# A decoder's self-attention with its projection groups in another place, some of its evictions on VectorE alone, and the first block's groups in another order

## The chip, the core and the metric

The kernel runs on one core of a Trainium2 chip. A core has five engines with a queue of instructions each: TensorE (PE; its weight loads are shown as PEld), VectorE (DVE), ScalarE (ACT), GpSimd (POOL) and SyncE (SP, which here issues all the transfers). Each works through its queue in order and waits at an instruction until semaphores of other engines or of transfers have come. The metric is the device time of one execution in microseconds (us); lower is better. Three runs of the kernel before gave 3051.44, 3047.96 and 3051.34 us; their median is 3051.34 us.

## The reference

A transformer encoder layer works on a context of 77 rows, and a decoder layer on 2048 rows, for 2 batches; width 512, 16 heads of 32 channels, feed-forward width 2048, all in float32. Cut to what matters here:

```python
x = src + mha(ln(src), ln(src), enc weights, eb);  memory = x + ff(ln(x))      # 77 rows a batch
yn = ln(tgt)                                                                    # 2048 rows a batch
y  = tgt + mha(yn, yn, dec_sa weights, rel_bias + causal)                       # the change is here
y  = y + mha(ln(y), memory, dec_ca weights, cb)
y  = y + relu(ln(y) @ ff1.T + b1) @ ff2.T + b2

def mha(xq, xkv, ...):
    q, k, v = xq @ wq.T + bq, xkv @ wk.T + bk, xkv @ wv.T + bv                  # 16 heads of 32
    attn = softmax(q @ k.T / sqrt(32) + bias)
    return (attn @ v) @ w_out.T + b_out
```

## The kernel before

The first part of the program, some 1865 us of it, is the decoder's self-attention, with the encoder and the first block's cross-attention fitted in between. The second part (cross-attention and feed-forward) is not touched by the change.

**Units, pieces, blocks.** The 2048 queries of a batch are cut into 4 *blocks* m of 512, numbered x = 0 to 7 over both batches (x = 4b + m); a block has 16 *units* (b, m, g, t): a group g of 4 heads and a tile t of 128 queries, in this order, so that there are 128 units n in all. By the causal mask tile i = 4m + t sees i + 1 tiles of 128 keys, which `pieces` (L292) cuts into pieces of at most four: one piece for m = 0, two for m = 1, three for m = 2, four for m = 3. The last piece of a unit has as many key tiles as are left: with m > 0 it is 2 for t = 0 and t = 1, 3 for t = 2 and 4 for t = 3.

A piece j of unit n passes through three steps:

- `scores(n, j)` (L325): four matmuls, one for each head, into four banks of PSUM. DVE evicts each bank to the buffer `pp` and takes the maximum (L352; L359 with the bias on the last two tiles); after the last piece DVE negates the maximum (L366) and ACT exponentiates each head's whole row (L367), four instructions a unit.
- `turn(n, j)` (L373): PE transposes the probabilities, 128x128 each (L387); every bank of four is copied to SBUF as `pts`, by ACT (L393), or, for the last piece of a unit, by DVE (L391; with one piece, ACT and DVE in turn). For the first piece the groups go by heads, so that the first waits for the first exponential alone; for later pieces they go by key tiles.
- `values(n, j)` (L396): PE multiplies the values with `pts` (L406) into a bank of its own, number 7. After the last tile of a head group ACT copies it out as `oT` (L412).

All other matmul groups take the seven other banks in turn (`bank`, L168).

**The projections.** For each block there are 16 jobs, each a group of 4 matmuls of 128x512 that the profile shows as 8: `q_job` (evicted by DVE, L206), `k_job` (evicted by ACT, L216), `v_job` (DVE, L229) and `out_job` (DVE, L241, and a store by SP). Small steps ("light") go with them: the loads, statistics, centring and the transposes of the next block's normal form (`norm_load`, `norm_stats`, `norm_center`, `norm_turn`; the four transposed tiles are scaled and shifted to `nT` by DVE and ACT in turn, L289 and L287), the division by the sums (`divide`), the encoder's 28 stages (one for each slot from 0 on, L942) and the first cross-attention (from slot 64 on, L956).

**What sets the order.** It is written out by hand. `jobs[n]` and `light[n]` list what goes into `slot(n)` (L948), at fixed distances from the block's first unit u = 16x (L877 to L903): a slot of a middle block has one job. The weights of a job are loaded by a transfer that is put into SP's queue earlier: two jobs are loaded at the start (L920), and each job that runs loads the next one of the list (L954), so that SP stands two jobs ahead. The last loop (L1199) gives the order of each engine's queue:

```python
for n in range(end):
    slot(n)
    for j in range(pn):
        turn(n, j)
        scores(n + 1, j + 1)     # or, for the last j: what unit n + 1 has more, and scores(n + 2, 0)
        values(n, j)
```

So the projection of slot n stands between `values` of the unit before and the first transposes of unit n. `scores(n + 1, k)` for k from pn on exist only where a unit has more pieces than the one before it: at the first unit of blocks 1, 2, 3, 5, 6 and 7.

Of the kernel before, what the change touches and what calls it, by code (L numbers as in the profile page):

```python
# [11 lines left out]
AF = mybir.ActivationFunctionType  # L12
ALU = mybir.AluOpType
# [7 lines left out]
NC = D // P  # L21
NF = DFF // P
HC = P // HD
MB = 512
# [30 lines left out]
def tile_encoder_decoder(ctx: ExitStack, tc: tile.TileContext, ins, out):  # L55
    nc = tc.nc
    x, src = ins["x"], ins["ctx_1024"]
# [19 lines left out]
    def vec(name, i):  # L77
        c = _COL[name] + i
        return vecs[:, c : c + 1]
# [67 lines left out]
    with (  # L147
# [6 lines left out]
        kT = ac.tile([P, NC, T], F32, name="kT")  # L154
# [13 lines left out]
        def bank():  # L168

            i = count["bank"] % count["banks"]  # L170
            count["bank"] += 1
            return psum[:, i, :]
# [13 lines left out]
        def small_w(c0, name="dec_sa_in_wT"):  # L186
            w = sb.tile([P, NC, P], F32, name="wqk", tag="wqk", bufs=3)
            nc.sync.dma_start(w, wchunk(name, c0, P))
            return w

        def big_w(kind, b, m):
            if wbig.get("is") != (kind, b, m):
                w = wbt
                nc.sync.dma_start(
                    w, wchunk("dec_sa_in_wT", 2 * D) if kind == "v" else wchunk("dec_sa_out_wT", 0)
                )
                wbig["is"], wbig["w"] = (kind, b, m), w
            return wbig["w"]

        def q_job(b, m, g):  # L200
            def run(w):
                mm = bank()
                for c in range(NC):
                    nc.tensor.matmul(mm, w[:, c, :], nTs[b, m][:, c, :], start=(c == 0), stop=(c == NC - 1))
                q = sb.tile([P, MB], F32, name="q", tag="q", bufs=3)
                nc.vector.tensor_scalar(q, mm, vec("dec_sa_in_b", g), SCALE, ALU.add, ALU.mult)  # L206
                qTs[b, m, g] = q

            return lambda: small_w(g * P), run

        def k_job(b, m, g):
            def run(w):
                mm = bank()
                for c in range(NC):
                    nc.tensor.matmul(mm, w[:, c, :], nTs[b, m][:, c, :], start=(c == 0), stop=(c == NC - 1))  # L215
                nc.scalar.activation(  # L216
                    kT[:, g, ts(m, MB)], mm, AF.Identity, bias=vec("dec_sa_in_b", NC + g)
                )

            return lambda: small_w(D + g * P), run  # L220

        def v_job(b, m, t):
            def run(w):
                mm = bank()
                for c in range(NC):
                    nc.tensor.matmul(
                        mm, nTs[b, m][:, c, ts(t, P)], w[:, c, :], start=(c == 0), stop=(c == NC - 1)
                    )
                nc.vector.tensor_tensor(vv[:, m * TB + t, :], mm, bv, ALU.add)  # L229

            return lambda: big_w("v", b, m), run
# [40 lines left out]
        def norm_turn(b, m, t, apart=False):  # L272
            xn = xs.pop((b, m, t))
            if t == 0:
                nTs[b, m] = nTt
            nT = nTs[b, m]

            pts = [bank()] * NC
            if apart:
                pts[0] = bank()  # L280
            for c in range(NC):
                nc.tensor.transpose(pts[c][:, ts(c, P)], xn[:, ts(c, P)], ident)
            for c in range(NC):
                d, pt = nT[:, c, ts(t, P)], pts[c]
                sc, bi = vec("dec_n1_s", c), vec("dec_n1_b", c)
                if c % 2 or (apart and c):
                    nc.scalar.activation(d, pt[:, ts(c, P)], AF.Identity, bias=bi, scale=sc)  # L287
                else:
                    nc.vector.tensor_scalar(d, pt[:, ts(c, P)], sc, bi, ALU.mult, ALU.add)  # L289
# [16 lines left out]
        units = [(b, m, g, t) for b in range(B) for m in range(NMB) for g in range(NC) for t in range(TB)]  # L306
# [66 lines left out]
        def turn(n, j):  # L373

            k0, kn = parts[n][j]
            p = state[n]["p"]
            pn = len(parts[n])
            got = {}
            if j == 0:
                order = [[(r, k) for k in range(kn)] for r in range(HC)]  # L380
            else:
                order = [[(r, k) for r in range(HC)] for k in range(kn)]
            for o, group in enumerate(order):
                pt = bank()
                pts = in_turn("pts", pts_all).rearrange("p (x q) -> p x q", q=P)
                for x, (r, k) in enumerate(group):
                    nc.tensor.transpose(pt[:, ts(x, P)], p[r][:, ts(k0 + k, P)], ident)  # L387
                    got[r, k] = pts[:, x, :]
                w = len(group) * P
                if j == pn - 1 and (pn > 1 or o % 2):  # L390
                    nc.vector.tensor_copy(pts[:, : len(group), :], pt[:, :w])  # L391
                else:
                    nc.scalar.copy(pts[:, : len(group), :], pt[:, :w])  # L393
            state[n]["pts"] = got
# [475 lines left out]
        jobs = {n: [] for n in range(-1, len(units) + NU)}  # L870
        light = {n: [] for n in range(-1, len(units) + NU)}

        for x, (b, m) in enumerate(blocks):
            u = x * NU
            first = m == 0

            jobs[u if first else max(u - 3, -1)].append(v_job(b, m, 0))  # L877
            jobs[u + 1 if first else u - 2].append(v_job(b, m, 1))
            jobs[u + 1].append(v_job(b, m, 2))
            jobs[u + 2].append(v_job(b, m, 3))  # L880
            jobs[max(u - 5, -1)].append(q_job(b, m, 0))
            jobs[max(u - 4, -1)].append(k_job(b, m, 0))
            jobs[max(u - 1, 0)].append(q_job(b, m, 1))
            jobs[u].append(k_job(b, m, 1))
            for g, at in ((2, 3), (3, 5)):
                jobs[u + at].append(q_job(b, m, g))
                jobs[u + at + 1].append(k_job(b, m, g))
            for t in range(TB):
                end = x == len(blocks) - 1
                jobs[u + NU + (2 if end else 7) + t].append(out_job(b, m, t))  # L890
                at = u + NU + ((-1, 0, 3, 4)[t] if end else 6 + t)
                light[at].append(lambda b=b, m=m, t=t: residual(b, m, t))
                if x:
                    light[u - NU + 4 + t].append(lambda b=b, m=m, t=t: norm_load(b, m, t))
                    light[u - NU + 5 + t].append(lambda b=b, m=m, t=t: norm_stats(b, m, t))
                    light[u - NU + 6 + t].append(lambda b=b, m=m, t=t: norm_center(b, m, t))
                    light[u - NU + 7 + t].append(lambda b=b, m=m, t=t: norm_turn(b, m, t))
            for g in range(NC):
                d = divide(b, m, g)
                for k in range(2):  # L900
                    light[u + g * TB + TB + k].append(lambda d=d: next(d, None))
                at = u + g * TB - 3
                light[max(at, -1)].append(lambda b=b, m=m, g=g: load_bias(b, m, g))  # L903
# [12 lines left out]
        def load_next():  # L916
            if len(loaded) < len(queue):
                loaded.append(queue[len(loaded)][0]())

        load_next()  # L920
        load_next()
        v = pp[:H, 13056 : 13056 + 3 * LT].rearrange("h (m u) -> h m u", u=LT)
        make_bias(1, rel, v)
        row_into(bv, "sa_bv")
# [23 lines left out]
        def slot(n):  # L948
            for f in light[n]:
                f()  # L950
            for _, run in jobs[n]:
                run(loaded[ran[0]])
                ran[0] += 1
                load_next()  # L954

        for r, fs in first_cross().items():  # L956
            light[len(units) // 2 + r] += fs


        w_1 = pp[:, : END // 2].rearrange("p (c o) -> p c o", c=NC)  # L960
# [235 lines left out]
            scores(0, j)  # L1196
        scores(1, 0)
        end = len(units)
        for n in range(end):  # L1199
            slot(n)  # L1200
            pn = len(parts[n])
            for j in range(pn):
                turn(n, j)
                if n + 1 < end:
                    nx = len(parts[n + 1])
                    if j < pn - 1:
                        if j + 1 < nx:
                            scores(n + 1, j + 1)
                    else:
                        for k in range(pn, nx):  # L1210
                            scores(n + 1, k)
                        if n + 2 < end:
                            scores(n + 2, 0)
                values(n, j)
# [61 lines left out]
```

## Time and profile before

| | |
|---|---|
| median of three runs | 3051.34 us (3047.96 to 3051.44) |
| profiled execution | 3047.41 us, span 3045.6 us, mean granted clock of TensorE 0.989 |
| self-attention, 0 to 1865.4 us of the span | PE busy 1803.09, DVE 1245.49, ACT 1122.47, POOL 91.24 us |
| the rest, 1865.4 to 3045.6 us | PE busy 1140.79, DVE 788.53, ACT 261.29, POOL 644.82 us |
| first transposes of blocks 0 to 7 | 46.7, 196.8, 424.0, 668.6, 979.9, 1118.0, 1326.2, 1570.8 us |

A row of the timeline gives start, duration, engine, line, instruction, tiles, shape and how many were merged; in square brackets stands the idle time of the engine before it and what ended it. A row of the waits gives engine, tile and line, what it waited for, then the sum, the number and the longest in us. A row of a table of stretches gives the length and, for PE, PEld, DVE, ACT and POOL, the busy time and in brackets the instructions, then the granted clock (1.00 is full) and the share and speed of the transfers. A matmul's end is modelled, so a PE row that is merged over a short wait counts that wait as busy: what PE loses is read from the starts.

### The profile page before, as it was taken

Reading aid. Unit: us, or ns where it says so; the run is one execution under the profiler, and the core shown is the slowest. Engines: PE = TensorE matmul, PEld = TensorE weight load, DVE = VectorE, ACT = ScalarE, POOL = GpSimd, SP = SyncE. Lnnn points to the kernel's source line nnn. Section 1 sums busy time; section 2 is a strip of 40 time slices with the busy share of each in tenths; the row PEclk is TensorE's granted clock in tenths of the full one; section 3 lists DMA queues with packets and bytes.
Section 4 is the critical chain, followed back from the end, with each engine's and each line's share of the span. In section 5 each row is a group of like instructions: output and inputs, shape, how many; then the busy total and the mean of one; then the engine's idle time right before and its main releaser. Section 6 shows DMA issues by size and latency. Waiting matters only on the chain. (4 is left out here: it accounts for less than half of the span.)

```text
span 3045.6 us, 60835 instructions
## 1 busy us (share of the span) xinstructions
PE 2943.9 (97%) x24440; PEld 2033.0 (67%) x24440; DVE 2034.0 (67%) x5863; ACT 1383.8 (45%) x2527; POOL 736.1 (24%) x601
## 2 busy tenths in 40 slices
PE   8899999999999999999999998999999999999999
PEld 5566656666665555656666665687778677778788
DVE  4766567766765777767666663676767666767765
ACT  2444466667776545566667773213131213131211
POOL 0100000000000101000000001464656454656465
PEclk9899999999999999999999999999999999999999
DMA  6413301201012421201101113200001000000000
GB/s 157 109 48 108 96 22 46 60 22 40 26 43 61 100 56 60 72 24 50 57 19 33 40 36 102 90 28 1 28 1 37 9 28 1 28 1 28 1 15 14
DMA packets 117644, 137.11 MB, mean 45 GB/s; under 512 B 18240, under 2 KB 73072, under 8 KB 117234
## 3 DMA queue, kind: packets, MB, share of 16 engines
q1 hardware_dynamic: 117362, 133.22, 15.3%
q8 instruction: 193, 3.16, 0.4%
q14 instruction: 89, 0.73, 0.1%
HBM read 111.33 MB, written 21.86 MB: 44 GB/s over the span
## 5 line engine op out<-in xcount | busy, mean ns | idle before, releaser
L352 DVE TENSOR_SCALAR_CACHE_REDUCE pp<-psum 128x512 f32<-128x512 f32 (+3 forms) x1024 | 560.6, 590 | 292.7 <-PE psum L343 292.7
L367 ACT ACTIVATE pp<-pp,nm 128x128 f32<-128x128 f32 (+15 forms) x512 | 610.6, 1194 | 152.3 <-DVE nm L366 149.5
L393 ACT COPY pts<-psum 128x512 f32<-128x512 f32 (+3 forms) x816 | 408.7, 581 | 418.9 <-PE psum L387 410.1
L387 PEld LDWEIGHTS psum<-ident,pp 128*128 128x128 f32 x4352 | 481.3, 142 | 119.7 <-issue 97.6
L387 PE MATMUL psum<-ident,pp 128*128 128x128 f32 x4352 | 544.6, 276 | 14.3 <-ACT pp L367 12.0
L1076 POOL TENSOR_TENSOR vv<-pp 128x512 f32<-128x512 f32 x320 | 413.0, 1307 | 149.2 <-PE psum L1093 129.9
L406 PEld LDWEIGHTS psum<-pts,vv 128*32 128x32 f32 x8704 | 219.0, 110 | 271.0 <-issue 146.4
L343 PE MATMUL psum<-kT,q 32*128 32x512 f32 (+3 forms) x2560 | 382.5, 579 | 4.6 <-ACT nT L287 1.6
L406 PE MATMUL psum<-pts,vv 128*32 128x128 f32 x8704 | 341.1, 279 | 30.8 <-DVE pts L391 28.1
L1112 ACT ACTIVATE kT<-kT,vecs 128x256 f32<-128x256 f32 x256 | 115.2, 499 | 322.3 <-DVE kT L1109 322.3
L359 DVE CUSTOM_DVE_ANT_0 pp<-psum,bias 128x256 f32<-128x256 f32 (+1 forms) x512 | 209.8, 410 | 60.0 <-PE psum L343 60.0
L264 POOL TENSOR_TENSOR rstd<-rstd,mhalf 128x1 f32<-128x1 f32 x32 | 18.5, 577 | 893.2 <-DVE rstd L263 893.2
L391 DVE COPY pts<-psum 128x512 f32<-128x512 f32 (+3 forms) x328 | 195.5, 645 | 52.8 <-PE psum L387 51.8
L1109 DVE TENSOR_TENSOR kT<-kT,psum 128x512 f32<-128x512 f32 x256 | 166.2, 679 | 83.1 <-PE psum L1093 83.1
L343 PEld LDWEIGHTS psum<-kT,q 32*128 32x128 f32 x2560 | 134.7, 183 | 81.8 <-issue 45.5
L1123 PE MATMUL psum<-vv 128*128 128x256 f32 x768 | 176.9, 381 | 0.0
L249 POOL TENSOR_TENSOR xr<-xr,row_dec_sa_out_b 128x512 f32<-128x512 f32 x32 | 40.9, 1280 | 525.5 <-DMA xr<-in_x_dram 246.7
L1093 PE MATMUL psum<-oT,vv 128*128 128x256 f32 x736 | 166.8, 380 | 0.0
L1123 PEld LDWEIGHTS psum<-vv 128*128 128x128 f32 x768 | 143.1, 190 | 26.8 <-issue 9.5
L1093 PEld LDWEIGHTS psum<-oT,vv 128*128 128x128 f32 x736 | 138.7, 190 | 24.8 <-issue 6.7
L1076 DVE TENSOR_TENSOR vv<-kT 128x512 f32<-128x512 f32 x160 | 140.9, 898 | 10.8 <-PE psum L1123 9.9
L215 PE MATMUL psum<-nT,wqk 128*128 128x512 f32 x256 | 120.3, 614 | 6.1 <-DMA wqk<-in_dec_sa_in_wT_dram 6.0
(167 smaller groups left out, 3922.8 us busy)
## 6 DMA issues: line engine op xcount, KB each, us to landing
wqk<-in_dec_sa_in_wT_dram SPq DMA_DIRECT2D x64, 256.0 KB, 4.3
bias<-tz SPq DMA_DIRECT2D x128, 128.0 KB, 3.6
wbig<-in_dec_sa_in_wT_dram SPq DMA_DIRECT2D x8, 1024.0 KB, 8.0
vv<-in_enc_ff_wT_dram SPq DMA_DIRECT2D x8, 1024.0 KB, 5.3
wbig<-in_dec_sa_out_wT_dram SPq DMA_DIRECT2D x8, 1024.0 KB, 10.0
xr<-in_x_dram SPq DMA_DIRECT2D x32, 256.0 KB, 4.5
y<-xr SPq DMA_DIRECT2D x32, 256.0 KB, 2.7
vv<-y SPq DMA_DIRECT2D x32, 256.0 KB, 3.5
```

Source lines behind the costliest of these rows:

```text
L343: nc.tensor.matmul(banks[r][:, : kn * P], q[rows4(r), ts(t, P)], kT[rows4(r), g, k0 * P : (k0 + kn) * P], start=True, stop=True,)
L352: nc.vector.tensor_scalar(p[:, k0 * P : (k0 + far) * P], s[:, : far * P], 1.0, None, ALU.mult, ALU.max, accum_out=st["mx"][:, r, c : c + 1],)
L359: nc.vector.tensor_tensor_reduce(p[:, (i + 1) * P - w : (i + 1) * P], s[:, far * P : kn * P], biases[b, m, g][:, r, 2 * P - w :], 1.0, LOW ...
L367: nc.scalar.activation(p[:, : (i + 1) * P], p[:, : (i + 1) * P], AF.Exp, bias=nm, accum_out=sums_of[b, m, g][:, t, r : r + 1],)
L387: nc.tensor.transpose(pt[:, ts(x, P)], p[r][:, ts(k0 + k, P)], ident)
L391: nc.vector.tensor_copy(pts[:, : len(group), :], pt[:, :w])
L393: nc.scalar.copy(pts[:, : len(group), :], pt[:, :w])
L406: nc.tensor.matmul(ot[rows4(r), t, :], vv[:, k0 + k, ts(g * HC + r, HD)], got[r, k], start=(k0 + k == 0), stop=(k0 + k == nb - 1),)
L1076: engine.tensor_tensor(dst, quarter(*parts[0], n), quarter(*parts[2], n), SIGN[parts[1]])
L1093: nc.tensor.matmul(mm[:, ts(f, TOK)], a[:, c, ts(f, P)], b[:, c, :], start=(c == 0), stop=(c == 1))
L1109: nc.vector.tensor_tensor(dst, dst, got, SIGN[sign])
L1123: nc.tensor.matmul(mm[:, t, :], lhs[:, c, ts(t, P)], rhs[:, c, :], start=(n == 0 and c == 0), stop=(n == 3 and c == 1),)
```

## The change

It does seven things: `slot(n + 1)` is called behind the last `turn` of unit n, ahead of the scores and the values that follow it, instead of ahead of unit n + 1; `norm_turn` leaves all four evictions to DVE (but for block 0); `k_job` evicts by DVE in blocks 2, 3, 6 and 7; the jobs of block 0 stand in other slots, and the v jobs of block 4 one or two slots later; three jobs are loaded at the start instead of two, so that the first v weights go into SP's queue ahead of the relative bias's write to DRAM; the two jobs of slot 4 load nothing, so that SP stands one job ahead from there on; and the first cross-attention begins one slot later.

```diff
@@ k_job
-                nc.scalar.activation(
-                    kT[:, g, ts(m, MB)], mm, AF.Identity, bias=vec("dec_sa_in_b", NC + g)
-                )
+                d, bi = kT[:, g, ts(m, MB)], vec("dec_sa_in_b", NC + g)
+                if m >= 2:
+                    nc.vector.tensor_scalar(d, mm, bi, None, ALU.add)
+                else:
+                    nc.scalar.activation(d, mm, AF.Identity, bias=bi)
@@ norm_turn
-                if c % 2 or (apart and c):
+                if apart and c:
                     nc.scalar.activation(d, pt[:, ts(c, P)], AF.Identity, bias=bi, scale=sc)
                 else:
                     nc.vector.tensor_scalar(d, pt[:, ts(c, P)], sc, bi, ALU.mult, ALU.add)
@@ the lists of jobs
-            jobs[u if first else max(u - 3, -1)].append(v_job(b, m, 0))
-            jobs[u + 1 if first else u - 2].append(v_job(b, m, 1))
-            jobs[u + 1].append(v_job(b, m, 2))
-            jobs[u + 2].append(v_job(b, m, 3))
+            jobs[u + 1 if first else max(u - 3, -1)].append(v_job(b, m, 0))
+            jobs[u + 2 if first else u - 2].append(v_job(b, m, 1))
+            jobs[u + 3 if first else u + 1].append(v_job(b, m, 2))
+            jobs[u + 4 if first else u + 2].append(v_job(b, m, 3))
             jobs[max(u - 5, -1)].append(q_job(b, m, 0))
             jobs[max(u - 4, -1)].append(k_job(b, m, 0))
-            jobs[max(u - 1, 0)].append(q_job(b, m, 1))
-            jobs[u].append(k_job(b, m, 1))
-            for g, at in ((2, 3), (3, 5)):
+            jobs[u - 1 if x else 2].append(q_job(b, m, 1))
+            jobs[u if x else 3].append(k_job(b, m, 1))
+            for g, at in ((2, 3), (3, 5)) if x else ((2, 4), (3, 5)):
                 jobs[u + at].append(q_job(b, m, g))
                 jobs[u + at + 1].append(k_job(b, m, g))
@@ the loads ahead
-        load_next()
-        load_next()
+        for _ in range(3):
+            load_next()
@@ slot
                 ran[0] += 1
-                load_next()
+                if n != 4:
+                    load_next()
 
         for r, fs in first_cross().items():
-            light[len(units) // 2 + r] += fs
+            light[len(units) // 2 + 1 + r] += fs
@@ the last loop
+        slot(0)
         for n in range(end):
-            slot(n)
             pn = len(parts[n])
             for j in range(pn):
                 turn(n, j)
+                if j == pn - 1 and n + 1 < end:
+                    slot(n + 1)
                 if n + 1 < end:
                     nx = len(parts[n + 1])
```

## The prediction

> **What bounds the kernel now.** First the head of the page, then the table of stretches for self-attention and for one middle block, then the waits.
>
> ```profile
> span 3045.6 us, 60835 instructions
> PE 2943.9 (97%) x24440; PEld 2033.0 (67%) x24440; DVE 2034.0 (67%) x5863; ACT 1383.8 (45%) x2527; POOL 736.1 (24%) x601
> ```
>
> ```profile
> 0.00:1865.40 1865.40, 1803.09 (x17880) 1140.93 (x17882) 1245.49 (x4510) 1122.47 (x2014) 91.24 (x98) 0.99 0.22 60
> 1326.20:1570.80 244.60, 241.13 (x2569) 152.61 (x2568) 170.12 (x612) 162.88 (x267) 7.23 (x8) 1.00 0.14 40
> ```
>
> ```profile
> PEld psum L406 <- DVE pts L391: 110.3, 174, 3.6
> PE psum L406 <- DVE pts L391: 28.1, 85, 3.3
> PE psum L387 <- ACT pp L367: 12.0, 13, 1.3
> PE psum L215 <- DMA wqk<-in_dec_sa_in_wT_dram: 6.0, 1, 6.0
> ```
>
> TensorE sets the end. Its 97% hides waits, because merged rows count short ones as busy; the weight loads of L406, which wait 110.3 us in 174 places for the copies of DVE, show them better. Block 2, unit 38 (t = 2, three key tiles in its last piece) in PE's timeline:
>
> ```profile
> 518.83 1.14 PE L343 MATMUL psum<-kT,q 32*128 32x512 f32 x8
> 519.90 1.08 PE L406 MATMUL psum<-pts,vv 128*32 128x128 f32 x32
> 520.91 1.53 PE L387 MATMUL psum<-ident,pp 128*128 128x128 f32 x12
> 522.37 2.20 PE L343 MATMUL psum<-kT,q 32*128 32x512 f32 x8
> 524.50 0.78 PE L406 MATMUL psum<-pts,vv 128*32 128x128 f32 x16
> 525.45 0.43 PE L406 MATMUL psum<-pts,vv 128*32 128x128 f32 x8 [0.17 <-DVE pts L391]
> 525.80 0.66 PE L282 MATMUL psum<-ident,xt 128*128 128x128 f32 x4
> 526.29 3.60 PE L238 MATMUL psum<-wbig,oT 128*128 128x512 f32 x8
> ```
>
> Undisturbed scores take 1.07 (518.83 to 519.90), those behind the last transposes 2.13; the values take 1.30 (524.50 to 525.80) where 24 of them take 0.79. PE loses 1.57 us, while DVE empties the score banks of the next unit and copies `pts`; then a projection of 3.44 us (8 x 0.43) follows that needs neither.
>
> **The projection moved (the main term).** It falls between the last transposes and the scores, so DVE has 3.44 us more before PE needs it. Read so, from start to start, units of blocks 2 and 6 lose 0.28, 1.09, 1.57 and 0.09 us there for t = 0 to 3: 3.03 a head group, 12.1 a block; the last unit, 1.4 more, and unit 40 bring it to 13.7. Slots 61, 62 and 123 to 127 have no job and give nothing back; the other units of blocks 1 to 7 lose, in this order, 13.3 + 13.7 + 11.6 + 11.5 + 12.2 + 13.7 + 7.5 = **83.5 us**. In block 0 units 6 to 10 are DVE's: 24.5 of 28 us busy between 100 and 128, where the wait only changes place; I take 3 there and read 4.5 in its other units: **7.5**.
>
> **Who waits next: ACT.** The first transposes now follow the values at once, and need the exponentials.
>
> ```profile
> 1683.43 1.88 ACT L367 ACTIVATE pp<-pp,nm 128x1920 f32<-128x1920 f32 x1
> 1685.22 0.18 ACT L367 ACTIVATION_READ_ACCUMULATOR pp<-pp,nm 128x1 f32 x1
> 1685.33 0.69 ACT L216 ACTIVATE kT<-psum,vecs 128x512 f32<-128x512 f32 x1
> 1685.92 2.04 ACT L393 COPY pts<-psum 128x512 f32<-128x512 f32 x4
> ```
>
> Unit 118's transposes start at 1685.13, its fourth head's group 1.31 later, 1.13 after the exponential's end (1685.31). The slot only moves within the same distance, so this slack shrinks just by the stall removed. In blocks 1 and 2 it is 2.8 us or more: nothing lost. In blocks 3 and 7 it is 1.1 to 1.7 for t = 2 and 3, against 1.09 and 1.57 removed; ACT's four copies (2.05) then start some 0.6 late and the values wait 0.55: eleven such units, **-6**. L412's copy (0.56) now runs in front of these copies without the projection to cover it: mostly inside their slack, **-1**.
>
> At the first units of blocks 1, 2, 3, 5, 6, 7 the unit's own last scores come behind the slot. Block 3: 0.95 from the scores to the first negated maximum, four exponentials at 1.67, L412, copies: 0.95 + 6.7 + 0.56 + 2.05 = 10.3, where the values would stand at 5.6 (scores 1.7, values 1.0, transposes 1.84, scores 1.07). That is 4.7, and 1.46 is lost there today: 3.3. In the same way 3.4 for m = 2 and 1.8 for m = 1; twice each: **-17**. The cover for this used to be the projection.
>
> **Evictions on DVE.** Normal form: 28 tiles, two more DVE instructions each of 0.407 (L289): 22.8 us of DVE, ACT rid of 56 x 0.456. Keys: 16 x 0.69 (L216, and L229 on DVE 0.687) = 11 us. The Trainium skill (TensorEngine Tiling (Array Packing), "PSUM Bottleneck") advises to evict with ScalarE and VectorE both; by it the change costs up to 22.8 + 11 = 34 us. The row says otherwise for the normal form: in one bank the two took turns, and ACT waited 40.0 us for L289, DVE 18.8 for L287. A tile held DVE 1.34 us with its wait (133.93 to 135.27, block 0); DVE starts its next instruction 0.33 after an L289 (115.41 to 115.73), so four come to 1.3 to 1.6. So DVE pays 0 to 8, and the key eviction stands where DVE waits for the projection anyway, as q's does. Were that cover gone: 11. With self-attention 66 us shorter DVE is 71% busy; in blocks 4 and 5 it goes from 75% to 81 to 85%, and I take **-5** (0 to -25). On ACT the key would have stood behind the four exponentials, and a bank with it.
>
> **Block 0's order.** Today PE waits 6.0 us for one k weight, and then runs at half clock:
>
> ```profile
> 34.55:40.52 5.97, 0.00 (x1) 0.04 (x1) 0.75 (x1) 0.00 (x0) 0.00 (x0) 0.89 0.92 200
> 40.52:46.91 6.39, 6.39 (x10) 2.76 (x11) 0.00 (x0) 0.00 (x0) 0.00 (x0) 0.57 0.01 2
> 107.50:110.90 3.40, 0.58 (x10) 0.19 (x5) 3.31 (x5) 0.01 (x1) 1.27 (x2) 0.99 0.00 0
> 110.90:117.70 6.80, 6.27 (x68) 5.04 (x69) 5.01 (x23) 3.98 (x12) 0.28 (x1) 0.50 0.77 86
> ```
>
> That job moves from slot 0 to slot 3. PE gets there near 50: first transposes done 27.8, v 3.4, scores to transposes 2.4, v, q and the encoder's transposes 7.5, again 3.2, the encoder's q 2.1, v 3.4. Its transfer, at 27.24 today, now stands behind the four bias pieces and a 768 KB bias write (8 us at the 95 GB/s of 9 to 15 us), with the 1 MB v weight gone from in front: landing 46 to 49. So **+8.8** (6.0, and 6.39 - 3.60; 5 if it lands late). The v weight passes SP's bias write and delays it by about 2 us; the first bias is needed at 25.7, its load lands near 25: 0 to -1.5, I take 0.
>
> New: in slot 5 the last q job stands directly behind k's, and, one job ahead only, its load stands in SP's queue behind a feed-forward weight that waits for the encoder's matmuls (L516) in the same slot. The like sequence today: L516 ends at 95.0, SP issues the three at 95.2, 95.9 and 96.3, and the small one is in near 101.2. So 6.2 after L516, of which k's projection covers 3.44: PE waits 2.8. The Trainium skill (TensorE: Matmul & The Clock Gate, "What's actually happening") halves the clock after a whole idle window of about 3.4 us; by it, 2.8. The rows above show half clock behind a stretch with 0.58 of 3.4 us still busy, so I add one such stretch, 1.7: **-4.5** (-2.8 to -6.2). Elsewhere the load one job ahead has a unit less a projection, 4 us or more, against a median landing of 4.3, and SP runs ahead; the 1 MB ones are gated by wbig's last reader, two slots earlier: 0. The later cross-attention and v jobs of block 4 move whole: 0.
>
> **Sum.** 83.5 + 7.5 - 6 - 1 - 17 - 5 + 8.8 - 4.5 = 66.3. The profiled execution took 3047.4 (span 3045.6 and 1.8 around it): 2981. The runs' median lies 3.9 above it, so **2985 us**.
>
> **Rivals.**
> - *The wait changes place.* For it: ACT's slack in blocks 3 and 7, DVE at 70% in order. Against: slacks of 2.8 to 20 us elsewhere. If blocks 2, 3, 6 and 7 gain nothing and pay the boundaries: 66.3 - 46.5 + 6 = 26, about 3025; with half of that loss, 3005.
> - *Slower: the loads one job ahead.* If each of the 16 q and k loads of the two one-piece blocks waited, as the first does today, and each wait brought a half-clock stretch, 16 x (2.8 + 1.7) = 72 makes 3057. It decides from 66.3 / 16 = 4.1 us each. Against: free buffers let SP issue early.
> - *The change does nothing*, since DVE is the true bound in order: against it, DVE idles 30% of the middle blocks. 3051.
> - *More than I take*: boundaries and DVE cost nothing: 66.3 + 22, 2963.
>
> **How the numbers follow.** Likeliest case 0.68, own range 2962 to 3000; wait changes place 0.20 (3000 to 3035); nothing 0.03; slower 0.09. 0.2%, 6 us, is what can be told from no change. Faster: 0.68 + 0.20 = 0.88; same 0.03; slower 0.09. The range that leaves 2 in 10 out: 2958 to 3026.
>
> **What would show it.** Scores behind the last transposes at 1.07 start to start in blocks 1 to 7, and the waits of L406 for L391 from 110 to under 25 us; the first transposes of blocks 2, 3, 6, 7 waiting for L367, some 3 us each; no wait for wqk near 35, one near slot 5; L289 at 4 in a row. The prediction is wrong if L387's waits for ACT grow by more than 40 us, if DVE is over 85% busy in a middle block, or if loads show up among PE's waits beyond slot 5.

## The result, and the profile after

The changed kernel takes 3013.33 us (median; 3010.93 to 3018.35) where the kernel before took 3049.22 on the same chip (3047.96 to 3051.44): ratio 0.9885, 95% interval 0.9871 to 0.9900. It is faster by 36 us, where the prediction had 66 (2985); 3013 lies inside the range of 2958 to 3026, outside the likeliest case's own 2962 to 3000 and within the 3000 to 3035 that the prediction gave, at 0.20, to its rival that the wait only changes place. The profiled execution took 3010.93.

The head of the page:

```profile
span 3009.2 us, 60899 instructions
PE 2913.9 (97%) x24440; PEld 2024.4 (67%) x24440; DVE 2057.2 (68%) x5935; ACT 1345.0 (45%) x2455; POOL 741.0 (25%) x601
```

PE is still the bound. DVE got 23 us more work, ACT 39 less. The table of stretches, for self-attention and for block 2 (duration, then busy time and instructions of PE, its weight loads, DVE, ACT and POOL, then granted clock, DMA share, GB/s):

```profile
0.00:1829.70 1829.70, 1773.11 (x17876) 1132.16 (x17876) 1277.91 (x4582) 1083.89 (x1942) 91.26 (x98) 0.98 0.22 61
1298.30:1534.80 236.50, 235.24 (x2573) 151.55 (x2569) 176.59 (x625) 157.27 (x257) 7.21 (x8) 1.00 0.14 41
```

The second row is block 6; block 2 takes the same 236.4, and both took 244.6 before. Self-attention's mean clock is 0.98, against 0.99. All that was won lies in self-attention: 1865.4 to 1829.7; the rest took 1180.3 and takes 1179.4. The waits:

```profile
PE psum L389 <- ACT pp L369: 20.6, 25, 1.3
...
PEld psum L408 <- DVE pts L393: 10.1, 14, 2.1
...
PEld psum L345 <- DVE pp L354: 5.8, 30, 0.3
...
PE psum L204 <- DMA wqk<-in_dec_sa_in_wT_dram: 4.0, 1, 4.0
PE psum L408 <- DVE pts L393: 3.9, 10, 1.8
...
PE psum L215 <- DMA wqk<-in_dec_sa_in_wT_dram: 2.7, 1, 2.7
```

The lines have moved by two: L387, L406, L343, L391, L367 and L352 are now L389, L408, L345, L393, L369 and L354. The values' waits for DVE's copies fell from 110.3 to 10.1 (weight loads) and 28.1 to 3.9 (matmuls). The first transposes wait longer for the exponentials (20.6 where it was 12.0). Two weights come late instead of one. New is the third of these lines: scores whose weight load waits for DVE's evictions of other scores, 30 places (2 before, 0.3 us). Unit 38 on PE again, followed by the start of unit 39:

```profile
510.13 1.53 PE L389 MATMUL psum<-ident,pp 128*128 128x128 f32 x12
511.50 0.60 PE L284 MATMUL psum<-ident,xt 128*128 128x128 f32 x4
511.94 3.60 PE L240 MATMUL psum<-wbig,oT 128*128 128x512 f32 x8
515.47 1.14 PE L345 MATMUL psum<-kT,q 32*128 32x512 f32 x8
516.54 0.86 PE L408 MATMUL psum<-pts,vv 128*32 128x128 f32 x24
517.33 2.00 PE L389 MATMUL psum<-ident,pp 128*128 128x128 f32 x16
519.26 2.10 PE L345 MATMUL psum<-kT,q 32*128 32x384 f32 x8
```

The projection (511.94) runs straight behind the last transposes; the scores after it take 1.07 and the values 0.79: the 1.57 us of before are gone. But the next piece's scores (519.26), three key tiles, take 2.03 up to the values at 521.29, where undisturbed ones take 0.86: that is the new wait, here 1.17 us, its longest form; in most places it is 0.2. DVE shows why it is long here:

```profile
514.53 1.36 DVE L291 TENSOR_SCALAR nT<-psum,vecs 128x128 f32<-128x128 f32 x4
515.80 0.54 DVE L272 TENSOR_SCALAR xt<-xt,bnmv,rstd 128x512 f32<-128x512 f32 x1
...
517.27 0.68 DVE L243 TENSOR_TENSOR xr<-psum,xr 128x512 f32<-128x512 f32 x1
517.87 0.68 DVE L354 TENSOR_SCALAR_CACHE_REDUCE pp<-psum 128x512 f32<-128x512 f32 x1
```

The small steps of the slot stand ahead of the scores' evictions in its queue, so that it begins to empty the first scores' banks at 517.87, 2.4 after those scores began (515.47).

By block (us between the first transposes of one block and of the next; blocks 3 to 5 together, because the later cross-attention and v jobs cross their borders):

| stretch | before | after | won | forecast |
|---|---|---|---|---|
| start to block 1 | 196.8 | 198.4 | -1.6 | +11.8 |
| block 1 | 227.2 | 216.2 | +11.0 | +11.5 |
| block 2 | 244.6 | 236.4 | +8.2 | +10.3 |
| blocks 3 to 5 | 657.6 | 647.3 | +10.3 | +22.2 |
| block 6 | 244.6 | 236.4 | +8.2 | +10.3 |
| block 7, to its last values | 294.5 | 295.0 | -0.5 | +1.2 |

The forecast column is the prediction's own terms sorted by block (blocks 1 and 5 pay 1.8 of the boundaries' 17, blocks 2 and 6 pay 3.4, blocks 3 and 7 pay 3.3 and 3 each of ACT's 6; the -5 stands in blocks 3 to 5; the -1 is in no block). Most of the missing 30 us is missing in two places: 13.4 before block 1, 11.9 in blocks 3 to 5. The times by block come from one profiled execution each. Kernels with the same work up to block 1 begin it at 197.0 to 201.2 (the changed one and experiments 3 and 7), so the first row, and what is read from it below, is good to some 2 us either way.

### The profile page after: what moved, and what is told of

It reads as the page before. It is cut to its first block, busy times and chain, and to the rows that moved or that the text cites. A ratio compares the mean times of both kernels' runs of the same rounds, so it can differ in the third digit from the quotient of the medians.

```text
span 3009.2 us, 60899 instructions
## 1 busy us (share of the span) xinstructions
PE 2913.9 (97%) x24440; PEld 2024.4 (67%) x24440; DVE 2057.2 (68%) x5935; ACT 1345.0 (45%) x2455; POOL 741.0 (25%) x601
## 5 line engine op out<-in xcount | busy, mean ns | idle before, releaser
L354 DVE TENSOR_SCALAR_CACHE_REDUCE pp<-psum 128x512 f32<-128x512 f32 (+3 forms) x1024 | 561.4, 590 | 247.0 <-PE psum L345 245.2
L369 ACT ACTIVATE pp<-pp,nm 128x128 f32<-128x128 f32 (+15 forms) x512 | 610.7, 1194 | 227.0 <-DVE nm L368 223.7
L389 PE MATMUL psum<-ident,pp 128*128 128x128 f32 x4352 | 562.9, 280 | 26.4 <-ACT pp L369 20.6
L389 PEld LDWEIGHTS psum<-ident,pp 128*128 128x128 f32 x4352 | 475.3, 142 | 103.2 <-issue 61.6
L1079 POOL TENSOR_TENSOR vv<-pp 128x512 f32<-128x512 f32 x320 | 419.4, 1326 | 150.1 <-PE psum L1096 130.4
L408 PEld LDWEIGHTS psum<-pts,vv 128*32 128x32 f32 x8704 | 225.1, 111 | 221.8 <-issue 186.5
L345 PE MATMUL psum<-kT,q 32*128 32x512 f32 (+3 forms) x2560 | 354.9, 584 | 3.0 <-ACT kT L220 1.6
L408 PE MATMUL psum<-pts,vv 128*32 128x128 f32 x8704 | 321.6, 280 | 7.2 <-DVE pts L393 3.9
L393 DVE COPY pts<-psum 128x512 f32<-128x512 f32 (+3 forms) x328 | 195.5, 645 | 30.3 <-PE psum L389 29.5
L345 PEld LDWEIGHTS psum<-kT,q 32*128 32x128 f32 x2560 | 123.3, 185 | 130.5 <-issue 82.0
```

The costliest lines, as they stand in the source:

```text
L345: nc.tensor.matmul(banks[r][:, : kn * P], q[rows4(r), ts(t, P)], kT[rows4(r), g, k0 * P : (k0 + kn) * P], start=True, stop=True,)
L354: nc.vector.tensor_scalar(p[:, k0 * P : (k0 + far) * P], s[:, : far * P], 1.0, None, ALU.mult, ALU.max, accum_out=st["mx"][:, r, c : c + 1],)
L369: nc.scalar.activation(p[:, : (i + 1) * P], p[:, : (i + 1) * P], AF.Exp, bias=nm, accum_out=sums_of[b, m, g][:, t, r : r + 1],)
L408: nc.tensor.matmul(ot[rows4(r), t, :], vv[:, k0 + k, ts(g * HC + r, HD)], got[r, k], start=(k0 + k == 0), stop=(k0 + k == nb - 1),)
L1079: engine.tensor_tensor(dst, quarter(*parts[0], n), quarter(*parts[2], n), SIGN[parts[1]])
```

## The experiments

Each time is a median held against the kernel before, run on the same chip beside it (3047.8 to 3050.9).

**1. The moved projection alone.** Normal form, keys, block 0's order and the loads are those of before:

```
-                if apart and c:
+                if c % 2 or (apart and c):
-                if m >= 2:
+                if m >= NMB:
...  jobs and loads of block 0 as before; batch 1's v jobs stay one slot later
```

> The projection group moved behind the last transposes, nothing else of the change but what that needs (batch 1's v jobs and the cross-attention one slot later); normal form and keys evicted as before, block 0's order and the loads as before. Theory A (the moved projection gives what the prediction says, and DVE's evictions and block 0's new order ate it): the prediction's terms without those two, 83.5 + 7.5 - 6 - 1 - 17 = 67, so about 2982. Theory B (what is missing went where the move itself puts it: first units of blocks, half clock, short blocks): 3005 to 3020, near the whole change at 3013.

Measured: 3030.98, ratio 0.9938 (0.9923 to 0.9953): 17 us won, neither 67 nor 36. By block against the whole change: block 1 216.2 as well, but block 2 241.2 (236.4), block 3 316.9 (306.0), block 6 239.6 (236.4). Theory A falls: without the evictions, which it took for a cost, more than half of the gain is gone. Theory B's range is missed as well (3005 to 3020), and its cause is in part excluded: block 6 takes 3.2 more, though it has no half clock in either kernel and the same place of the projection in both.

**2. The normal form in turns again, all else as changed.** The first of the two edits above, alone.

> The changed kernel with the normal form's four tiles evicted by VectorE and ScalarE in turns again. By the prediction (and the rule of two engines) it is 0 to 5 faster than the changed kernel's 3013: 3008 to 3013. Rival, read from the run of the move alone, whose blocks 2, 3 and 6 took 4.8, 10.9 and 3.2 longer than the whole change's: a bank that ScalarE holds behind its exponentials stops the transposes and scores after it, and a good part of these 19 belongs to the normal form: 3017 to 3027.

Measured: 3030.31, ratio 0.9946 (0.9927 to 0.9966): 17 us slower than the changed kernel. The prediction's -5 has the wrong sign. From this kernel's waits:

```profile
DVE nT L291 <- ACT nT L289: 38.6, 28, 4.3
```

And from its timelines of ACT, DVE and PE, the slot behind unit 54's last transposes:

```profile
788.31 1.99 ACT L369 ACTIVATE pp<-pp,nm 128x2048 f32<-128x2048 f32 x1
790.29 0.44 ACT L289 ACTIVATE nT<-psum,vecs 128x128 f32<-128x128 f32 x1
...
790.76 0.41 DVE L291 TENSOR_SCALAR nT<-psum,vecs 128x128 f32<-128x128 f32 x1 [3.71 <-ACT nT L289]
...
791.72 0.66 PE L389 MATMUL psum<-ident,pp 128*128 128x128 f32 x4 [1.61 <-ACT nT L289]
```

ACT's tile stands in its queue behind four exponentials of 1.99 each. DVE, whose next tile is in the same bank, waits 3.71 for it, with all that is queued behind it on DVE: the next row's centering and statistics, and the scores' evictions. PE then waits for the bank. Before the change DVE waited 18.8 us in as many places (28, longest 1.8) and the projection, standing between the values and the next transposes, covered it. With the projection moved the waits are 38.6 and nothing covers them: blocks 2 and 6 take 3.3 more, block 3 10.0. That ACT merely has more to do is not the cause: the transposes wait 21.1 us for its exponentials here, as in the changed kernel (20.6). Whether it would help to split the work by banks, and not inside one, was not tried.

**3. The keys on ScalarE again, all else as changed.** The second edit alone.

> The changed kernel with all keys evicted by ScalarE again. By the prediction's pricing of the keys on VectorE (inside a wait, at most 11, part of -5) no slower than the changed kernel: 3008 to 3014. Rival, from the same 19 us of the run of the move alone: the key stands behind four exponentials in the long blocks and a bank with it: 3018 to 3030. This and the run with the normal form in turns should add to about 19 if the two parts are independent.

Measured: 3013.92, ratio 0.9885 (0.9868 to 0.9901). No difference, and blocks 2, 3 and 6 take 236.4, 305.3 and 236.4 as in the changed kernel: the rival falls. What experiment 1 lacked was the normal form.

**4. The evictions without the move.** Both eviction edits in the kernel before.

> The kernel before with the normal form and the long blocks' keys evicted by VectorE alone, and nothing else of the change. Putting the normal form back in turns cost the changed kernel 17. Theory A (these 17 are a price that only the moved projection would have to pay; in the old order the projection stands between ScalarE's late tile and the next transposes and hides it): 3043 to 3051, no change to 6 faster. Theory B (the eviction is worth its 17 by itself): 3030 to 3035. The prediction's own pricing: 3052 to 3054.

Measured: 3043.53, ratio 0.9976 (0.9966 to 0.9985): 7 us won. Theory A's range just holds it, B's does not: most of the 17, but not all, is a price that only the moved projection pays. In which blocks the 7 are won the traces don't show, since the two profiled executions, 3046.31 and 3047.41, are 1.1 apart. The move alone wins 17, the evictions alone 7; both together, with block 0's order as before (experiment 5), win 40. Some 15 us belong to the pair, an estimate from four medians.

**5. Block 0's jobs in the old order, two loads ahead; all else as changed.**

```
-        for _ in range(3):
-            load_next()
+        load_next()
+        load_next()
-                if n != 4:
-                    load_next()
+                load_next()
...  q, k and v jobs of block 0 in the slots of before
```

> The changed kernel with block 0's jobs in the order of before, two loads at the start, two jobs ahead throughout. By the prediction the new order is worth 8.8 - 4.5 = 4.3, so 3017. Rival (block 0 is DVE's, and a start 19 us earlier only brings its work to DVE sooner; the new order gives nothing and costs the wait in slot 5): 3003 to 3011.

Measured: 3008.20, ratio 0.9870 (0.9851 to 0.9888). By the medians the new order costs 5 where the prediction had it bring 4.3; but the four runs lie from 3003.89 to 3015.34, the intervals overlap with the changed kernel's, and the profiled run is the fastest of the four. In its trace block 1 starts at 193.4, where the kernels with the new order have 197.0 to 201.2. So the order brings nothing as it stands; that it costs 5 is likely and not shown. (Experiment 1 differs from this one by the evictions alone, 22.8, of which the normal form is 17.)

**6. No load left out.** The second edit of experiment 5 alone: three jobs ahead throughout.

> The changed kernel with loads three jobs ahead throughout, none left out at slot 4. By the prediction the wait in slot 5 (2.8 forecast, 4.0 in the trace) and the half clock behind it (1.7) go: 3007 to 3009. Rival (block 0 is DVE's, PE only waits later): 3012 to 3014.

Measured: 3003.72, ratio 0.9854 (0.9837 to 0.9870); 9.6 less than the changed kernel, whose interval begins where this one ends; block 1 starts at 189.9, 8.5 earlier. Slot 5's last q projection in PE's timeline, changed kernel (first fence) and this one:

```profile
91.18 5.32 PE L204 MATMUL psum<-nT,wqk 128*128 128x512 f32 x8 [3.98 <-DMA wqk<-in_dec_sa_in_wT_dram]
```

```profile
87.10 3.60 PE L204 MATMUL psum<-nT,wqk 128*128 128x512 f32 x8
```

The prediction saw this wait, with its half-clock stretch (5.32 where this run takes 3.60). The other 2.7 us, L215's wait in the list of waits, comes near 190, with block 1's second k job: it too has only one job's lead, and it goes in this run as well.

**7. Own last scores first.** At a block's first unit the unit's own last scores go ahead of the projection:

```
-                if j == pn - 1 and n + 1 < end:
-                    slot(n + 1)
                 if n + 1 < end:
+                    if j == pn - 1:
+                        for k in range(pn, len(parts[n + 1])):
+                            scores(n + 1, k)
+                        slot(n + 1)
...
-                        for k in range(pn, nx):
-                            scores(n + 1, k)
```

> The changed kernel, but at a block's first unit the projection stands behind that unit's own last scores, in front of the scores of the unit after. By the prediction's term for the first units (17) and the half clock that follows the wait in blocks 3 and 7 (two stretches of 6.8, 3.4 each): blocks 1, 2, 3, 5, 6, 7 each 2 to 7 shorter, in all 15 to 24: 2990 to 2998. Rival (ACT's exponentials are as late as before, and PE only waits one place further on): under 4, 3010 to 3013.

Measured: 2994.50, ratio 0.9821 (0.9807 to 0.9836): 19 us faster than the changed kernel. By block: 1.6, 2.7, 3.7, 1.8, 2.7 and 5.1 shorter in blocks 1, 2, 3, 5, 6 and 7, together 17.6: the prediction's term of 17. Block 3's first unit in the changed kernel shows what these units pay, first in PE's timeline, then in the table of stretches:

```profile
652.61 0.66 PE L389 MATMUL psum<-ident,pp 128*128 128x128 f32 x4 [0.95 <-ACT pp L369]
654.27 1.11 PE L389 MATMUL psum<-ident,pp 128*128 128x128 f32 x4 [1.01 <-ACT pp L369]
...
656.99 2.09 PE L345 MATMUL psum<-kT,q 32*128 32x512 f32 x8
```

```profile
651.00:654.30 3.30, 1.34 (x13) 0.86 (x9) 2.11 (x8) 3.30 (x5) 0.00 (x0) 1.00 0.00 0
654.30:661.10 6.80, 6.25 (x49) 3.53 (x50) 2.01 (x7) 3.99 (x7) 0.00 (x0) 0.50 0.00 0
```

The transposes wait for each exponential and take 4.1 us more than undisturbed ones, of which half clock on the last of them is a part; 6.8 us run at half clock. The scores behind them take 2.0 instead of 1.07, which is not the clock's doing alone: in the kernel before they took 1.99 at full clock,

```profile
670.62 2.06 PE L343 MATMUL psum<-kT,q 32*128 32x512 f32 x8
672.61 1.47 PE L406 MATMUL psum<-pts,vv 128*32 128x128 f32 x32
```

and the values after them 1.40, where the changed kernel has 1.87. With its own scores first, the same unit waits 1.4 us in all at these transposes and stays at full clock:

```profile
645.20:648.50 3.30, 2.29 (x25) 1.75 (x19) 1.66 (x6) 3.30 (x6) 0.00 (x0) 1.00 0.12 36
648.50:655.30 6.80, 6.80 (x98) 4.41 (x98) 3.52 (x11) 3.76 (x8) 0.00 (x0) 1.00 0.01 2
```

**8. Both mends together** (experiments 6 and 7).

> The changed kernel with a block's first unit putting its own last scores ahead of the projection and with no load left out at slot 4. If the two costs are independent, 18.8 + 9.6 off the changed kernel's 3013: 2985. Rival (block 0's half clock or DVE gives part of it back): 2990 to 2995.

Measured: 2985.07, ratio 0.9794 (0.9779 to 0.9808). The two costs add up, as far as these runs can tell, and this is the fastest version: 64 us below the kernel before. That it meets the predicted figure is chance; its blocks don't meet the forecast's.

**9. The short blocks as before.** The projection moves only where the coming unit is in a long block; blocks 0 and 4 have the order, jobs and loads of before:

```
-                if j == pn - 1 and n + 1 < end:
+                early = n + 1 < end and units[n + 1][1] > 0
+                if early and j == pn - 1:
                     slot(n + 1)
...
                 values(n, j)
+            if not early and n + 1 < end:
+                slot(n + 1)
```

> The projection moved only where the coming unit lies in blocks 1, 2, 3, 5, 6, 7; in the two short blocks (0 and 4) the order of work, the jobs and the loads are those of before. To be held against the changed kernel with block 0's jobs in the old order (3008). Theory A (in the short blocks VectorE sets the end, the wait only changes place): 3004 to 3012. Theory B (the prediction's 7.5 in block 0 and 11.5 in block 4 were earned by the move and lost to something else): about 19 more, 3022 to 3030.

Measured: 3009.85, ratio 0.9871 (0.9856 to 0.9886), against 3008.20 in experiment 5, which differs in the place of the projection in these blocks and what hangs on it. Theory A's number: in the two short blocks the move is worth nothing that these runs resolve, where the prediction counted 7.5 and 11.5. Unit 8 of block 0 in the changed kernel, on PE's timeline and in two stretches, shows where a wait went:

```profile
128.33 0.33 PE L389 MATMUL psum<-ident,pp 128*128 128x128 f32 x1 [3.04 <-DVE mx L361]
```

```profile
124.00:130.60 6.60, 3.34 (x36) 2.35 (x24) 6.21 (x23) 2.52 (x9) 2.79 (x2) 0.85 0.11 39
128.60:145.70 17.10, 15.92 (x87) 10.68 (x87) 14.98 (x67) 8.28 (x26) 4.05 (x2) 0.50 0.01 1
```

DVE is busy for 6.21 of 6.60 us; PE waits for it at the first transposes, 3.04 in one piece, where in the kernel before it waited behind the last ones (the scores behind unit 8's transposes took 5.4 us there), and runs at half clock for the next 17.1 us. In block 4 the waits reappear too, 1.8 us at unit 69's transposes and 3.0 in the cross-attention's scores of unit 78 (4.0 for 1.06), behind which 3.4 us run at half clock. But DVE is busy there for 104.6 of 140.6 us only: that it sets block 4's end is not shown, and by what order of DVE's and ACT's work those waits come was not taken apart.

**10. The projection between scores and values,** block 0's order as in experiment 5:

```
-                if j == pn - 1 and n + 1 < end:
-                    slot(n + 1)
...
                             scores(n + 2, 0)
+                        slot(n + 1)
                 values(n, j)
```

> The changed kernel with block 0's jobs in the old order (3008), but the projection stands between the scores and the values instead of ahead of both. Theory A (the scores' part of the wait behind the last transposes, 57 of the 85 us in blocks 1 to 7 of the kernel before, is a wait for banks and comes back; the values' part stays hidden; the second scores get their 3.4 us of distance to the first scores' evictions back, so L345's waits for L354, 5.8 us in 30 places, go; the first units gain as where their own last scores went first, 17): 3008 + 50 - 6 - 17 = 3035. Theory B (any place behind the last transposes does, DVE only needs the time before the values): 2985 to 2995.

Measured: 3022.04, ratio 0.9911 (0.9891 to 0.9930), 14 slower than experiment 5. Theory A's mechanism, its size too large by 13. The scores behind the last transposes wait again (42 us in blocks 1 to 7, read as in the prediction: 1.06 at t = 2, 0.22 at t = 1), the first units are cured, and the new wait is gone:

```profile
PEld psum L345 <- DVE pp L354: 0.5, 3, 0.2
```

30 places became 3. The edit changes two things for these waits: with 3.44 us of projection between the first scores and the second, DVE has emptied the banks in time; in the changed order only values and first transposes lie between, 2.9 us (1.01 and 1.90) against DVE's 2.5 for four evictions (4 x 0.61), and DVE often starts them late, as at 517.87 above. The slot's small steps now also stand behind the first scores' evictions in DVE's queue, and which of the two does more was not taken apart. All waits between scores and values, other than behind the last transposes, are 8.4 us before, 21.7 in the changed kernel and 5.6 here.

## Why the prediction was right and wrong

**The main term, 83.5: right in size, wrong in two places.** Read as the prediction read it, from start to start against undisturbed work of the same shape, the loss behind the last transposes in blocks 1 to 7 went from 86 us to 6. In the long blocks that became time. In block 4 (11.5 of the term) and in block 0 (7.5) it did not: the prediction named DVE as the limit in units 6 to 10 of block 0, left 3 us there, and let block 4's part stand whole. By experiment 9 the move brings the two blocks together 1.7 us, less than the runs resolve. The rival "the wait changes place" was therefore true, but of blocks 0 and 4, and hardly of 2, 3, 6 and 7, for which it was written: blocks 2 and 6 gained 8.2 each and block 3 5.3; block 7, with 1.2 forecast, lost 0.5. So the range held the time because it was wide enough to take in this rival; that the time falls within the rival's own 3000 to 3035 is in part luck, since other blocks lost it and other terms than the place of the wait had their share.

**ACT, -6: right in cause, a little too small.** In blocks 3 and 7 the units with t = 2 lose 0.27 at the first transposes and 0.24 at the values, those with t = 3 0.17 and 0.24: 0.4 to 0.5 each, nine units, 4.2 us, where the prediction had eleven at 0.55. The count leaves out unit 63, behind the two units of block 3 that have no job: it loses 4.2 more than before (2.2 at its first transposes, 1.3 at the values, 0.6 at the next transposes), by waits for ACT and 3.4 us at half clock behind them. There the wait did change place.

**The first units, -17: right.** Experiment 7 returns 18.8, 17.6 of it in the blocks named. Unit 32 loses 3.41 (1.98, 0.34 and 0.39 at transposes, scores and values, 0.70 at the scores ahead), where the prediction had 3.4. Block 3's first unit loses 6.65, or 5.2 more than the 1.46 of before, against 3.3. Not in the sum were the 0.70 at the scores ahead and the half clock; the rest of the 1.9 was not taken apart.

**L412 and what follows it, -1: the missed term.** What was missed is not L412's copy but the banks. The prediction asked who waits for ACT when the projection goes, and not which banks the second scores need. They were 3.44 us closer to the first scores' evictions than before. The waits there grew by 13 us in blocks 1 to 7, some 3 of it in the first units already counted: about 10.

**Evictions on DVE, -5: wrong sign.** The prediction priced what DVE must do more, and set the rule of using both engines (the Trainium skill, TensorEngine Tiling (Array Packing), "PSUM Bottleneck") against the row that showed the two taking turns. The row was the right one, but only half was read from it: ACT's place in the turn is behind four exponentials, 8 us in block 3, and the cover for that was the projection that the change takes away. The tile that the prediction timed (1.34) was one of block 0, where an exponential takes 0.62; in block 3 it takes 1.99. Leaving the normal form in turns costs 17 (experiment 2); by the rule it would have gained up to 23. Blocks 4 and 5, for which the -5 stood, take as long with either form (140.8 and 200.4 against 140.6 and 200.6). The keys' price of nothing was right (experiment 3).

**Block 0's order, +8.8 - 4.5: right at the start, too small in slot 5.** PE comes to the first transposes 19.4 us earlier (27.3 against 46.7) with three jobs of 3.44 still to do: 9.1 gained, where 8.8 was forecast. In experiment 6, which has only this part of the new order, 4.5 of it is left against experiment 5 by the medians, 3.5 by the start of block 1, neither clear of the noise. Block 0 gives back the rest; two of its projections run at half clock (1.58 and 1.80 too long), but the old order has half clock there too, so that this is not shown to be the cause. The load left out costs 9.6 instead of 4.5 (bounds 2.8 to 6.2): the wait itself was 4.0 for 2.8, and a second one came, 2.7 in slot 16. That a load one job ahead has "4 us or more" elsewhere and costs 0 was the failing step: the rival of late loads was right in two places, where it needed 16. Loads beyond slot 5 were one of the three signs named for a wrong prediction; the other two did not come (L389's waits for ACT grew by 8.6 us, 25 with those of its weight loads, and DVE is busy for 75% of blocks 2, 4 and 6).

Together: the short blocks 17, the second scores 10, the left-out load 5, what block 0 gave back 4, less the 5 that DVE didn't cost. These make 31 against 30 missing, but they overlap in block 0, unit 63's loss and the half clock are in none of them, and what block 0 gave back is not clear of the noise: the agreement is no proof of each share. How much is the clock's own part was not measured apart: from the first transposes on, self-attention ran at half clock for 27 us before and 65 after, so at most half of the 38, an estimate, if PE set the end in all of them.

## What to carry to other kernels

When a job is moved to cover one stall, ask what it covered where it was: here an eviction that two engines shared, banks that a second group of matmuls needed, and the exponentials of a block's first unit. A share of an engine's work belongs with the engine whose queue is short at that moment; a tile in a queue behind 8 us of exponentials holds up the other engine and the bank. In stages that another engine bounds, count a removed stall as nothing until a run shows otherwise, and look at the granted clock behind the wait that takes its place.

## What was unexpected of the hardware

The granted clock fell to half behind stretches in which PE still worked: 1.34 us of 3.3 before the 6.8 us stretch at 654.3, transposes for the most part, and 0.58 of 3.4 in the prediction's row, scores and values. The stretches at half clock are 3.4 us or whole multiples of it (6.8, 17.1). The Trainium skill (TensorE: Matmul & The Clock Gate, "What's actually happening") has the clock drop after a whole idle window; here less than that was enough. How much less is not shown. In block 3 PE stood idle for about as long in both kernels, 8.5 us before and 9.5 after by its busy times, yet ran 6.8 us at half clock before and 13.7 after. So the sum of the waits doesn't tell how much runs at half clock; what this cost in time was not measured apart.
